# Row maxima of a two-layer cross attention: one turning product for both query halves, at another place in each slot

## Chip, cores and metric

The kernel runs on one core of one Trainium2 chip. The metric is the device time of one execution in microseconds (us). The kernel before took 1475.73 us in the median of three runs (1470.49 to 1479.28).

## What is computed

Two cross-attention layers follow each other over 16 sequences of 256 queries with 320 channels (20 heads of 16). Keys and values come from a context of 256 tokens with 512 channels, of which some are text tokens and some image tokens: 77 and 179 in layer 1, 252 and 4 in layer 2. Text and image have softmaxes of their own, so each query has a row maximum for each part and head.

```python
def layer1(x, ctx, mask):                          # text = ctx[:, :77], ip = ctx[:, 77:]
    q = x @ Wq                                     # [16, 256, 320], 20 heads of 16
    probs  = softmax(q_h @ k_text_h.T * scale)     # over the 77 text tokens, each head
    sem    = softmax(q @ k_text.T * scale) @ text @ ip.T * scale    # all heads together
    ip_p   = softmax(q_h @ k_ip_h.T * scale + 0.5 * sem) * mask     # over the 179 image tokens
    return (probs @ v_text_h + ip_p @ v_ip_h) @ Wout + bout + x

def layer2(x, ctx, mask):                          # text = ctx[:, :-4], ip = ctx[:, -4:]
    probs  = softmax(q_h @ k_text_h.T * scale)     # over the 252 text tokens
    qsem   = l2norm(probs @ text)                  # for each head
    ip_p   = softmax(q_h @ k_ip_h.T * scale + 0.5 * qsem @ l2norm(ip).T) * mask
    return (probs @ v_text_h + ip_p @ v_ip_h) @ Wout + bout + x

out = layer2(layer1(x, ctx, mask), ctx, mask)
```

## The kernel before

Four heads of one sequence are a group; there are 5 groups a sequence, so 80 groups in layer 1 (k from 0 to 79) and 80 in layer 2 (k from 80 to 159; NS is 80). The main loop runs over slots, one a group; a slot works on several groups at once, at different stages. Between its fixed steps a slot calls `fill`, which takes steps from other tasks (projections, keys, values, output) by a table of due times; these are the rows of the lines L260, L632, L690 and L1108.

A layer 1 slot k does, in this order on TensorE (PE):

- `maxima0(k + 1)`: the row maxima of the next group are turned so that they lie along a row. Each of the two halves of 128 queries has its own product with an identity matrix (L780), 8 rows by 128 columns. ScalarE (ACT) copies both halves into the tile `mt` (L782, 8 x 256), and a DMA on ACT's queue writes them into two rows of the group's stacked queries `Q` (L783).
- `score0(k + 2, 0)`: the scores of the first half (L772), and their row maxima on VectorE (DVE), one reduction for text and one for image (L773 and L774). They go to the tile `mn`. The scores' PSUM tile S exists once.
- `turned0(k, 0)`: the scores once more, keys on the rows, for half the keys (L795). The rows of `Q` with the maxima take part in this product, so that the maximum is subtracted in it. ACT takes the exponential (L798) and GpSimd (POOL) multiplies by the semantic factor (L801).
- a `fill`, then `attend0(k - 1)`: 24 products with the values of the group before (L833), each on a quarter of the array's columns.
- `score0(k + 2, 1)` and `turned0(k, 1)` for the second halves, then two more `fill`s. `stacks(k + 4, "KQ")` behind them has the SP queue load keys and queries of a later group (L83).

Layer 2 is alike. In slot k `both1(k, t)` does the probabilities of group k (L917, with the row of maxima in it) and the scores of group k + 2 (L922, maxima L923), for t = 0 and t = 1, with `attend1(k - 2)` (L988 and L990) between the two. Behind them come four blocks `norm1` (L975), `rounded1` (L965, L966) and the fills, and at the slot's end `maxima1(k + 2)`: two products (L955), a copy (L957) and a DMA (L959).

PE's order is the order in which the program is written. In layer 1 a scheduler sets the order on ACT, DVE, POOL and the SP queue, within the few fixed orders that `queued` and `anchor` add; `turned0` has the second half's exponentials queued behind the DMA of the next group's maxima, and `stacks(..., "M")` has a copy queued behind the latest copy of maxima. In layer 2 ACT, DVE and POOL follow the program too. `bank()` gives one of three PSUM banks (X) in turn.

Of the kernel before, what the change touches and what calls it, by code (L numbers as in the profile page):

```python
# [9 lines left out]
FR = mybir.dt.float32r  # L10
AF = mybir.ActivationFunctionType
ALU = mybir.AluOpType
AX = mybir.AxisListType
# [4 lines left out]
S = 256  # L18
# [6 lines left out]
T0 = 77  # L25
NIP = 4
BI = B * NIP
T1 = S - NIP
# [21 lines left out]
def xattn2(  # L50
# [39 lines left out]
    def bank(tag="X"):  # L90
        return ps.tile([128, 512], F32, tag=tag, name=tag, bufs=BANKS[tag])
# [83 lines left out]
    def anchor(inst):  # L175
        anchors[inst.ins.engine] = inst
        return inst
# [587 lines left out]
    def score0(k, t):  # L765
        Q, K = QK[k]
        if t == 0:
            maxes[k] = buf("mn", [128, 2, 2, 4], FR, bufs=2)
        mn = maxes[k]
        sp = scores()  # L770
        for h in range(4):
            mm(sp[:, h], Q[: XROW + T0, h, t * 128 : (t + 1) * 128], K[: XROW + T0, h], start=True, stop=True)  # L772
        nc.vector.tensor_reduce(mn[:, t, 0], sp[:, :, :T0], axis=AX.X, op=ALU.max)  # L773
        anchor(nc.vector.tensor_reduce(mn[:, t, 1], sp[:, :, T0:], axis=AX.X, op=ALU.max))  # L774

    def maxima0(k, queue=nc.scalar):
        Q, mn = QK[k][0], maxes[k]
        mp = bank()
        for t in range(2):
            mm(mp[:8, t * 128 : (t + 1) * 128], mn[:, t].rearrange("p a h -> p (a h)"), ident_r, start=True, stop=True)  # L780
        mt = buf("mt", [8, S], FR)
        casts.append(nc.scalar.copy(mt, mp[:8, :S]))  # L782
        issues[k] = queue.dma_start(f(Q[KS0 - 2 : KS0]), f(mt))  # L783

    def turned0(k, t):
# [17 lines left out]
    def attend0(k):  # L803
        b, g = divmod(k, NG)
        v, pv = get("v0", b), bank("P")
        for vt in range(3):
            values0(k, pv, v, vt)
        settle0(b, g, pv)

    def slot0(k):  # L810
        if k > 0:
            yield lambda: maxima(k + 1)
            yield lambda: stacks(k + LEAD - 1, "M")
        yield lambda: ahead(k + 2, 0)
        yield lambda: turned0(k, 0)
        yield 0.2
        if k == 2:
            yield lambda: stacks(k + LEAD - 1, "KQ")
        if k > 0:
            yield lambda: attend0(k - 1)  # L820
            yield lambda: stacks(k + LEAD - 1, "T")
        yield lambda: ahead(k + 2, 1)
        yield lambda: turned0(k, 1)
        if k != 1:
            yield lambda: stacks(k + LEAD, "KQ")
        yield 0.6
        yield 1.0
# [75 lines left out]
    def both1(k, t):  # L903

        a = k + 2 < 2 * NS and QK[k + 2] 
        c = NS <= k < 2 * NS and QK[k]
        if a:
            if t == 0:
                maxes[k + 2] = buf("mn", [128, 4, 4], FR, bufs=2)[:, :2]
            sp = scores()  # L910
        if c:
            st = [bank("T").rearrange("p (h t) -> p h t", h=2) for u in range(2)]
            lo = (0, DUP)[t]
            for j in range(2):
                for u in range(2):
                    rows = slice(64 * u, 64 * u + KS1)
                    mm(st[u][:, j], c[1][rows, j, lo : lo + 128], c[0][rows, j], start=True, stop=True)  # L917
        if a:
            for j in range(2):
                for u in range(2):  # L920
                    rows = slice(64 * u, 64 * u + XROW)
                    mm(sp[:, 2 * u + j], a[0][rows, j, t * 128 : (t + 1) * 128], a[1][rows, j], start=True, stop=True)  # L922
            anchor(nc.vector.tensor_reduce(maxes[k + 2][:, t], sp[:, :, :T1], axis=AX.X, op=ALU.max))  # L923
            image_scores(k + 2 - NS, t, sp)
        if c:
            for u in range(2):
                if t == 0:
                    P[k, u] = buf("P", [128, 2, 2, S], bufs=SIZES["NP"]) if (k - NS) % 3 else last_stack([128, 2, 2, S], F32, u)
                anchor(nc.scalar.activation(P[k, u][:, t], st[u], AF.Exp, scale=SCALE))  # L929
# [20 lines left out]

    def maxima1(k):
        mn = maxes[k]
        mp = bank()
        for t in range(2):
            mm(mp[:4, t * 128 : (t + 1) * 128], mn[:, t], ident_r, start=True, stop=True)  # L955
        mt = buf("mt", [8, S], FR)[:4]
        nc.scalar.copy(mt, mp[:4, :S])  # L957
        row = QK[k][0].rearrange("(u p) j t -> u p j t", u=2)[:, XROW]
        late(lambda: nc.scalar.dma_start(f(row), f(mt)))  # L959

# [32 lines left out]
    def slot1(k):  # L993
        last = k - 1 if NS < k <= 2 * NS else None
        mine = k < 2 * NS
        if k == NS:
            yield lambda: maxima(k + 1)
        yield lambda: both1(k, 0)
        if k == NS:
            yield lambda: attend0(k - 1)  # L1000
# [2 lines left out]
            yield lambda: summed.append(attend1(k - 2))  # L1003
        yield release
        yield lambda: both1(k, 1)
        if last:
            yield lambda: norm1(last, 0, 0)
        yield 0.2
# [14 lines left out]
        if mine:  # L1023
            yield lambda: rounded1(k, 1)
        yield 0.8
        yield lambda: maxima(k + 2)
        yield lambda: stacks(k + LEAD)
        yield 1.0

# [248 lines left out]
    def maxima(k):  # L1278
        if k < 2 * NS:
            (maxima0 if k < NS else maxima1)(k)  # L1280
# [189 lines left out]
```

## Time and profile before

| | |
|---|---|
| time before | 1475.73 us median of 3 runs (1470.49 to 1479.28) |
| the profiled execution | 1475.7 us, its span 1475.7 us |
| PE busy | 1433.6 us (97%), 12438 matmuls |
| DVE, POOL, ACT busy | 1166.0 us (79%), 1151.8 us (78%), 956.5 us (65%) |
| TensorE clock | granted in full in all 40 slices |
| DMA engines | busy 50.3% of the span for the SP queue's transfers, 0.2% for ACT's |

In the profile PE's rows are matmuls and PEld's their weight loads; a row gives the start, the length from the start of the first to the end of the last of the merged instructions, and how many these were. Matmuls are pipelined: the ends are modelled, and what one costs is read from the start of one to the start of the next. `[0.41 <-issue]` at a row's end is idle time of that engine ahead of it, and what ended it. ACTq and SPq rows are DMAs that these engines issue; q10 is ACT's DMA queue.

### The profile page before, as it was taken

Reading aid. Unit: us, or ns where it says so; the run is one execution under the profiler, and the core shown is the slowest. Engines: PE = TensorE matmul, PEld = TensorE weight load, DVE = VectorE, ACT = ScalarE, POOL = GpSimd, SP = SyncE. Lnnn points to the kernel's source line nnn. Section 1 sums busy time; section 2 is a strip of 40 time slices with the busy share of each in tenths; the row PEclk is TensorE's granted clock in tenths of the full one; section 3 lists DMA queues with packets and bytes.
Section 4 is the critical chain, followed back from the end, with each engine's and each line's share of the span. In section 5 each row is a group of like instructions: output and inputs, shape, how many; then the busy total and the mean of one; then the engine's idle time right before and its main releaser. Section 6 shows DMA issues by size and latency. Waiting matters only on the chain.

```text
span 1475.7 us, 35302 instructions
## 1 busy us (share of the span) xinstructions
PE 1433.6 (97%) x12438; PEld 1186.7 (80%) x12438; DVE 1166.0 (79%) x2569; ACT 956.5 (65%) x2074; POOL 1151.8 (78%) x1173
## 2 busy tenths in 40 slices
PE   6899999999999999799999999999999999999998
PEld 6788888888888878687778887888888888888865
DVE  5487676777677787967888888888888888888897
ACT  5577676767676776756666566656665666566553
POOL 4179797979797877987788877787778877887785
PEclk9999999999999999999999999999999999999999
DMA  6756565656656577565434433543354345433511
GB/s 196 194 160 184 134 184 141 184 143 165 162 154 164 144 195 205 140 184 158 138 102 140 146 119 101 161 146 102 118 161 146 89 131 161 135 101 116 150 32 50
DMA packets 230667, 211.78 MB, mean 144 GB/s; under 512 B 56314, under 2 KB 217116, under 8 KB 230492
## 3 DMA queue, kind: packets, MB, share of 16 engines
q1 hardware_dynamic: 229222, 208.56, 50.3%
q8 instruction: 99, 1.62, 0.5%
q10 hardware_dynamic: 1270, 0.98, 0.2%
q14 instruction: 76, 0.62, 0.1%
HBM read 122.07 MB, written 86.44 MB: 141 GB/s over the span
## 4 chain that ended last, share of the span: by engine, by line
PE 86%; DMA 4%; DVE 3%; POOL 3%; ACT 2%; issue 1%; SPq 0%; ACTq 0%; DVEq 0%; POOLq 0%
PE X L260 22%; PE X L975 18%; PE X L632 11%; PE P L833 7%; PE S L772 5%; PE P L988 5%; PE T L917 5%; PE T L795 4%; PE S L922 3%; PE P L990 2%; DMA kd<-kst 2%; PE X L1108 1%; POOL P L801 1%; PE X L690 1%; POOL wt L966 1%
## 5 line engine op out<-in xcount | busy, mean ns | idle before, releaser
L801 POOL TENSOR_TENSOR P<-P,rs 128x512 f32<-128x512 f32 x320 | 413.6, 1316 | 140.2 <-ACT P L798 140.2
L975 PE MATMUL X<-ctb,gm 128*128 128x512 f32 x1120 | 295.3, 407 | 0.0
L966 POOL TENSOR_TENSOR wt<-P,ctb 128x512 f32<-128x512 f32 x212 | 268.6, 1296 | 0.0
L923 DVE TENSOR_REDUCE mn<-S 128x4 fp32r<-128x1008 f32 x160 | 192.8, 1205 | 81.0 <-PE S L922 79.4
L975 PEld LDWEIGHTS X<-ctb,gm 128*128 128x128 f32 x1120 | 203.6, 190 | 49.4 <-issue 0.4
L798 ACT ACTIVATE P<-T 128x512 f32<-128x512 f32 x320 | 174.7, 593 | 100.5 <-PE T L795 81.0
L978 DVE TENSOR_TENSOR wt<-X,wt 128x512 f32<-128x512 f32 x240 | 159.3, 681 | 4.9 <-PE X L975 4.9
L929 ACT ACTIVATE P<-T 128x512 f32<-128x512 f32 x212 | 115.0, 597 | 54.5 <-PE T L917 41.6
L980 POOL TENSOR_TENSOR wt<-wt 128x512 f32<-128x512 f32 x80 | 103.6, 1295 | 58.3 <-DVE wt L978 58.3
L965 ACT ACTIVATE ctb<-P 128x512 fp32r<-128x512 f32 x212 | 122.5, 625 | 32.7 <-PE X L975 31.1
L774 DVE TENSOR_REDUCE mn<-S 128x4 fp32r<-128x716 f32 x160 | 142.4, 890 | 0.0
L833 PE MATMUL P<-P,vr 128*32 128x256 f32 x1920 | 123.8, 387 | 1.8 <-DVE tmp L850 0.8
L632 PE MATMUL X<-hq,wE 128*128 128x256 f32 x768 | 111.1, 289 | 4.4 <-ACT hq L615 3.9
L260 PE MATMUL X<-cta,wA 128*128 128x252 f32 (+3 forms) x726 | 104.2, 289 | 6.9 <-ACT wA L187 6.8
L632 PE MATMUL X<-ho,wF 128*128 128x256 f32 x768 | 106.6, 284 | 0.9 <-DVE ho L871 0.6
L632 PEld LDWEIGHTS X<-hq,wE 128*128 128x128 f32 x768 | 101.6, 195 | 7.2 <-ACT hq L615 4.4
L260 PEld LDWEIGHTS X<-cta,wA 128*128 128x128 f32 (+1 forms) x726 | 94.4, 191 | 10.7 <-ACT wA L187 7.0
L632 PEld LDWEIGHTS X<-ho,wF 128*128 128x128 f32 x768 | 98.7, 189 | 3.9 <-DVE ho L871 1.0
L844 DVE STREAM_TRANSPOSE nt<-P 128x512 f32<-128x512 f32 x80 | 57.0, 713 | 44.2 <-PE P L833 43.9
L773 DVE TENSOR_REDUCE mn<-S 128x4 fp32r<-128x308 f32 x160 | 74.5, 466 | 21.5 <-PE S L772 21.1
L833 PEld LDWEIGHTS P<-P,vr 128*32 128x32 f32 x1920 | 55.7, 110 | 42.7 <-issue 6.0
L772 PE MATMUL S<-ks,qs 125*128 125x256 f32 x480 | 87.0, 304 | 0.9 <-DVE mn L774 0.8
(223 smaller groups left out, 3279.7 us busy)
## 6 DMA issues: line engine op xcount, KB each, us to landing
qd<-q SPq DMA_DIRECT2D x48, 384.0 KB
kd<-kst SPq DMA_DIRECT2D x66, 256.0 KB
rawc<-in_cT_dram SPq DMA_DIRECT2D x60, 256.0 KB
qs<-qd SPq DMA_DIRECT2D x160, 96.0 KB
ks<-kd SPq DMA_DIRECT2D x160, 96.0 KB
qs<-qd SPq DMA_DIRECT2D x60, 192.0 KB
ks<-kd SPq DMA_DIRECT2D x60, 192.0 KB
qd<-q SPq DMA_DIRECT2D x32, 256.0 KB
```

The source lines that it names most:

```text
L260: last = mm(out, lhs(a, k), rhs(b, k), start=i == 0, stop=i == len(terms) - 1)
L632: mm(pp, w(s, k, slice(m * 128, (m + 1) * 128)), a[:, t], start=i == 0, stop=i == len(terms) - 1)
L772: mm(sp[:, h], Q[: XROW + T0, h, t * 128 : (t + 1) * 128], K[: XROW + T0, h], start=True, stop=True)
L774: anchor(nc.vector.tensor_reduce(mn[:, t, 1], sp[:, :, T0:], axis=AX.X, op=ALU.max))
L798: exp = anchor(nc.scalar.activation(pt, st[p], AF.Exp, scale=SCALE))
L801: anchor(nc.gpsimd.tensor_mul(pt, pt, rs[:, t : t + 1].to_broadcast([128, 2, S])))
L833: mm(pv[32 * s : 32 * s + 32, o : o + S], v[:, vt, h : h + 32], P[k, s // 2][:, t, s % 2], start=vt < 2, stop=vt != 1,)
L923: anchor(nc.vector.tensor_reduce(maxes[k + 2][:, t], sp[:, :, :T1], axis=AX.X, op=ALU.max))
L965: nc.scalar.activation(R[k, u][:, t], P[k, u][:, t], AF.Copy, scale=0.5)
L966: anchor(nc.gpsimd.tensor_sub(W[k, u][:, t], P[k, u][:, t], f(R[k, u][:, t])))
L975: mm(yp, gm[:, gb], R[k, u][:, kt], start=i == 0, stop=i == len(blocks[n]) - 1)
L978: nc.vector.tensor_mul(product, yp, w[:, n])
```

## The change

The maxima tile gets the half of the queries as its last index, so that both halves' maxima lie next to each other. One product turns both: 16 rows by 128 columns in layer 1, 8 by 128 in layer 2, in place of two products of 8 and of 4 rows. The copy has 128 columns instead of 256 on twice the rows, and the DMA twice as many rows of half the length (16 of 512 bytes in layer 1). In layer 1 `maxima(k + 1)` moves from the head of slot k to the place directly behind `attend0(k - 1)`, past the first scores, the first probabilities and a fill. In layer 2 the maxima of group k + 1 are turned in slot k directly behind `both1(k, 1)`; before, they were turned at the end of slot k - 1.

```diff
     def score0(k, t):
...
-            maxes[k] = buf("mn", [128, 2, 2, 4], FR, bufs=2)
+            maxes[k] = buf("mn", [128, 2, 4, 2], FR, bufs=2)
...
-        nc.vector.tensor_reduce(mn[:, t, 0], sp[:, :, :T0], axis=AX.X, op=ALU.max)
-        anchor(nc.vector.tensor_reduce(mn[:, t, 1], sp[:, :, T0:], axis=AX.X, op=ALU.max))
+        nc.vector.tensor_reduce(mn[:, 0, :, t], sp[:, :, :T0], axis=AX.X, op=ALU.max)
+        anchor(nc.vector.tensor_reduce(mn[:, 1, :, t], sp[:, :, T0:], axis=AX.X, op=ALU.max))
 
     def maxima0(k, queue=nc.scalar):
         Q, mn = QK[k][0], maxes[k]
-        mp = bank()
-        for t in range(2):
-            mm(mp[:8, t * 128 : (t + 1) * 128], mn[:, t].rearrange("p a h -> p (a h)"), ident_r, start=True, stop=True)
-        mt = buf("mt", [8, S], FR)
-        casts.append(nc.scalar.copy(mt, mp[:8, :S]))
+        mp = bank()[:16, :128]
+        mm(mp, mn.rearrange("p a h t -> p (a h t)"), ident_r, start=True, stop=True)
+        mt = buf("mt", [16, 128], FR)
+        casts.append(nc.scalar.copy(mt, mp))
         issues[k] = queue.dma_start(f(Q[KS0 - 2 : KS0]), f(mt))
 
     def slot0(k):
         if k > 0:
-            yield lambda: maxima(k + 1)
             yield lambda: stacks(k + LEAD - 1, "M")
...
             yield lambda: attend0(k - 1)
+            yield lambda: maxima(k + 1)
             yield lambda: stacks(k + LEAD - 1, "T")
...
     def maxima1(k):
         mn = maxes[k]
-        mp = bank()
-        for t in range(2):
-            mm(mp[:4, t * 128 : (t + 1) * 128], mn[:, t], ident_r, start=True, stop=True)
-        mt = buf("mt", [8, S], FR)[:4]
-        nc.scalar.copy(mt, mp[:4, :S])
+        mp = bank()[:8, :128]
+        mm(mp, mn.rearrange("p c t -> p (c t)"), ident_r, start=True, stop=True)
+        mt = buf("mt", [8, 128], FR)
+        nc.scalar.copy(mt, mp)
...
     def slot1(k):
...
-        if k == NS:
-            yield lambda: maxima(k + 1)
         yield lambda: both1(k, 0)
...
         yield lambda: both1(k, 1)
+        yield lambda: maxima(k + 1)
...
         yield 0.8
-        yield lambda: maxima(k + 2)
         yield lambda: stacks(k + LEAD)
```

Behind the change the line numbers are one to four lower (L779 for L780, L794 for L795, L832 for L833; L916, L921, L953 and L973 for L917, L922, L955 and L975). PE's order in one layer 1 slot, before: from the last values of group k - 1 (L833, `v` on `P`) to the next slot's probabilities (L795, on the queries `qs_188`). L772 are scores into S, L690 is a fill's step, L780 turns the maxima.

```order
L833 MATMUL P<-P_93,vr 32x256 x2
L833 MATMUL P<-P_94,vr 32x256 x2
L772 MATMUL S<-ksl,qsl 128x256 x4
L795 MATMUL T<-qs_187,ks_191 128x256 x4
L690 MATMUL X<-kb_238,q_297 128x192 x12
L780 MATMUL X<-ident_r,mn_556 8x128 x2
L772 MATMUL S<-ks_190,qs_186 128x256 x4
L795 MATMUL T<-qs_188,ks_192 128x256 x4
```

The same place on PE after the change:

```order
L832 MATMUL P<-P_93,vr 32x256 x2
L832 MATMUL P<-P_94,vr 32x256 x2
L779 MATMUL X<-ident_r,mn_555 16x128
L772 MATMUL S<-ksl,qsl 128x256 x4
L794 MATMUL T<-qs_187,ks_191 128x256 x4
L690 MATMUL X<-kb_238,q_297 128x192 x12
L772 MATMUL S<-ks_190,qs_186 128x256 x4
L794 MATMUL T<-qs_188,ks_192 128x256 x4
```

The product that fills the maxima row of `qs_188` stood a slot's length ahead of the probabilities that read it; it now stands behind the values, with the second half's scores and probabilities, the fill and one more block of scores between.

ACT's order in the same slot, before: P are exponentials, `qs_186<-tph` and `ks_191<-M` copies for later groups, `mt` the turned maxima.

```order
L782 CAST mt_196<-X 8x256
L744 CAST ks_190<-M_333 77x4x179
L798 ACTIVATE P_95<-T 128x512
L783 DMA qs_188<-mt_196 2x4x256
L798 ACTIVATE P_96<-T 128x512
L741 CAST qs_186<-tph_449 77x1024
L798 ACTIVATE P_95<-T 128x512
L798 ACTIVATE P_96<-T 128x512
```

After, the same rows on ACT:

```order
L744 CAST ks_190<-M_333 77x4x179
L445 ACTIVATE M_332<-X 77x179
L429 ACTIVATE vr<-X,tmask 128x20x16
L797 ACTIVATE P_95<-T 128x512
L797 ACTIVATE P_96<-T 128x512
L741 CAST qs_186<-tph_449 77x1024
L781 CAST mt_196<-X 16x128
L782 DMA qs_188<-mt_196 2x8x128
L797 ACTIVATE P_95<-T 128x512
L797 ACTIVATE P_96<-T 128x512
```

The copy of the maxima and its DMA have gone from ahead of the first half's exponentials to between the first half's and the second half's, behind the copy of `tph`.

PE in a layer 2 slot, before, from the second scores (L922) to the next slot's probabilities (L917); L975 are the blocks of `norm1`:

```order
L922 MATMUL S<-ks_190,qs_186 128x256 x4
L975 MATMUL X<-ctb_82,gm 128x512 x4
L632 MATMUL X<-hq_293,wE_85 128x256 x8
L975 MATMUL X<-ctb_82,gm 128x512 x3
L975 MATMUL X<-ctb_83,gm 128x512 x7
L955 MATMUL X<-ident_r,mn_555 4x128 x2
L260 MATMUL X<-cta_80,wA_84 128x252 x6
```

And after:

```order
L921 MATMUL S<-ks_190,qs_186 128x256 x4
L953 MATMUL X<-ident_r,mn_556 8x128
L973 MATMUL X<-ctb_82,gm 128x512 x4
L632 MATMUL X<-hq_293,wE_85 128x256 x8
L973 MATMUL X<-ctb_82,gm 128x512 x3
L973 MATMUL X<-ctb_83,gm 128x512 x7
L260 MATMUL X<-cta_80,wA_84 128x252 x6
```

The pair has left the stream of full-array products at the slot's end, and the one product that is left stands where the array changes from the 48-row products L921 to full ones.

More of the change, by code (lines that the diff above doesn't have):

```diff
@@ L908, in both1 @@
             if t == 0:
-                maxes[k + 2] = buf("mn", [128, 4, 4], FR, bufs=2)[:, :2]
+                maxes[k + 2] = buf("mn", [128, 4, 2], FR, bufs=2)
             sp = scores()
@@ L922, in both1 @@
                     mm(sp[:, 2 * u + j], a[0][rows, j, t * 128 : (t + 1) * 128], a[1][rows, j], start=True, stop=True)
-            anchor(nc.vector.tensor_reduce(maxes[k + 2][:, t], sp[:, :, :T1], axis=AX.X, op=ALU.max))
+            anchor(nc.vector.tensor_reduce(maxes[k + 2][:, :, t], sp[:, :, :T1], axis=AX.X, op=ALU.max))
             image_scores(k + 2 - NS, t, sp)
```

## Prediction

> **What bounds the kernel now.** I read the page first, then the groups by line and shape, the waits, and the timeline of a slot in each layer. On the page, the span and the chain of work that ended last:
>
> ```profile
> span 1475.7 us, 35302 instructions
> ...
> PE 86%; DMA 4%; DVE 3%; POOL 3%; ACT 2%; issue 1%; SPq 0%; ACTq 0%; DVEq 0%; POOLq 0%
> ```
>
> 86% of the chain is PE: what is taken out of PE's stream comes off the time, unless a wait takes its place. The groups of the turning products, by line and shape:
>
> ```profile
> L780 PE MATMUL X<-ident_r,mn 128*8 128x128 f32 x160 | 24.8, 225 | 5.1 <-DVE mn L774 3.7 <-DMA kd<-kst 0.3 <-DVE ho L871 0.3
> ...
> L955 PE MATMUL X<-ident_r,mn 128*4 128x128 f32 x160 | 22.9, 223 | 0.6 <-DVE kst L564 0.6
> ```
>
> There are 160 of each, 80 pairs a layer. Their means of 0.22 us are modelled ends; what a pair costs is in the starts. PE's timeline at the end of a layer 2 slot and in the next:
>
> ```profile
> 1004.15 0.28 PE L955 MATMUL X<-ident_r,mn 128*4 128x128 f32 x2
> 1004.27 2.12 PE L632 MATMUL X<-ho,wF 128*128 128x256 f32 x16
> 1006.23 1.12 PE L632 MATMUL X<-hq,wE 128*128 128x256 f32 x8
> ...
> 1011.08 1.11 PE L632 MATMUL X<-hq,wE 128*128 128x256 f32 x8
> 1012.03 2.49 PE L975 MATMUL X<-ctb,gm 128*128 128x512 f32 x10
> ```
>
> In a stream, eight L632 take 1012.03 - 1011.08 = 0.95, so 0.119 us each. The pair takes 1004.27 - 1004.15 = 0.12, and the sixteen L632 behind it 1006.23 - 1004.27 = 1.96 where 16 x 0.119 = 1.90: their first weights wait behind the small ones. A pair thus costs 0.12 + 0.06 = 0.18 us.
>
> **The change part by part.** *One product for two, and its new place.* The slot of layer 1 that the order shows, in the timeline:
>
> ```profile
> 316.94 1.50 PE L833 MATMUL P<-P,vr 128*32 128x256 f32 x24
> ...
> 317.30 1.03 ACT L741 CAST qs<-tph 77x1024 fp32r<-77x1024 f32 x1
> 318.37 0.54 PEld L772 LDWEIGHTS S<-ksl,qsl 125*128 125x128 f32 x4 [0.41 <-issue]
> 318.37 0.74 PE L772 MATMUL S<-ksl,qsl 125*128 125x256 f32 x4
> ...
> 318.95 0.64 PE L795 MATMUL T<-qs,ks 127*128 127x256 f32 x4
> ...
> 319.45 1.09 ACT L798 ACTIVATE P<-T 128x512 f32<-128x512 f32 x2 [1.12 <-PE T L795]
> ...
> 319.62 0.30 SPq L83 DMA_DIRECT2D ks<-kd  x1
> ...
> 320.13 2.54 POOL L801 TENSOR_TENSOR P<-P,rs 128x512 f32<-128x512 f32 x2 [0.59 <-ACT P L798]
> ...
> 320.75 0.28 PE L780 MATMUL X<-ident_r,mn 128*8 128x128 f32 x2
> ...
> 321.07 0.36 ACT L782 CAST mt<-X 8x256 fp32r<-8x256 f32 x1
> ...
> 321.39 0.64 PE L795 MATMUL T<-qs,ks 127*128 127x256 f32 x4
> ...
> 321.46 0.62 ACTq L783 DMA_DIRECT2D qsl<-mt  x1
> ...
> 322.91 0.85 PE L833 MATMUL P<-P,vr 128*32 128x256 f32 x12
> ```
>
> Behind the values the weight path stands still for 0.41 us while the array changes over, and the scores then start with an exposed load. The product now stands in that gap. No row has it there. The nearest is a pair whose second half waited for DVE, so that its load started on a weight path that stood idle:
>
> ```profile
> 307.25 0.09 PEld L780 LDWEIGHTS X<-ident_r,mn 128*8 128x8 f32 x1 [0.34 <-DVE mn L774]
> 307.32 0.53 PEld L772 LDWEIGHTS S<-ks,qs 125*128 125x128 f32 x4
> ```
>
> The scores' load follows 0.07 us after the small one; alone it would have started at 307.25. I take 0.07 for the product there. The bounds are 0 (it fits into the 0.41) and half a pair in the stream and all of the load's delay, 0.06 + 0.06 = 0.12. In layer 2 the place is of the same kind, since there too a full load follows products that use part of the array, and I take 0.07 again. A slot saves 0.18 - 0.07 = 0.11 us, at the bounds 0.06 and 0.18.
>
> *Where the saving doesn't count.* Rows of the waits, then of what the probabilities of layer 2 wait for:
>
> ```profile
> PEld S L772 <- issue: 30.5, 73, 0.8
> ...
> PEld X L780 <- DVE mn L774: 7.4, 11, 1.7
> ...
> PE T L795 <- DMA qs<-mt: 4.6, 1, 4.6
> ...
> PE X L780 <- DVE mn L774: 3.7, 4, 1.4
> ```
>
> ```profile
>   ACT P L929: 6.2, 15
>   DVE sr L939: 5.3, 13
> ```
>
> The first row says that the gap behind the values is there in 73 slots. In 11 + 4 = 15 slots the pair waited for the reduction L774. The scores behind it write the PSUM tile S, which exists once and which that reduction reads, so the wait stays and changes its name to the scores': nothing is saved there. In layer 2, 15 + 13 = 28 slots start with a wait for ACT or DVE, and I count them as nothing too. Layer 1: 65 x 0.11 = 7.2 us. Layer 2: 52 x 0.11 = 5.7 us. Together 12.9 us, at the bounds 117 x 0.06 = 7 and 117 x 0.18 = 21.
>
> The Trainium skill ("TensorE: Matmul & The Clock Gate", section "LDWEIGHTS (loading the stationary operand)") has a load take its number of columns divided by 1.2 GHz, 0.013 us for 16 columns; by that the product would cost some 0.02 us in the gap and the sum would come to an estimated 117 x 0.16 = 19 us. The trace doesn't bear it out for small loads: 8 columns show 0.09 us, and the next load 0.07 later.
>
> *The later transfer in layer 1.* This is what speaks against the change. The maxima of the next group were on their way a whole slot ahead; now the chain product, copy, issue, landing has to fit between the values and the next slot's probabilities. In the slot above the product starts at 318.37. ACT's copy of `tph`, which the order puts ahead, ends at 317.30 + 1.03 = 318.33 and is out of the way. Copy: 0.32 after the first product as at 321.07, so 318.69, and 0.36 long at most (half the columns). Issue: 0.39 after the copy's start as at 321.46, so 319.08. The landing is seen in ACT's queue q10. All ten of its packets of the issue at 321.46 lie in the window from 321.46 to 322.95:
>
> ```profile
> q10 hardware_dynamic: 10, 0.01, 1.6%
> ```
>
> That is 1.49 us at most, so the row is there at 320.57; twice the rows of half the length I put at 0 to 0.2 more. It is read by L795, which would start at 321.39 - 0.18 + 0.07 = 321.28. So 0.5 to 0.7 us are left. Of the 77 slots that I followed from the values to the next slot's probabilities, 18 are about as tight (2.9 to 3.0 us from scores to probabilities), the first and the last of them with these probabilities:
>
> ```profile
> 157.13 0.64 PE L795 MATMUL T<-qs,ks 127*128 127x256 f32 x4
> ```
>
> ```profile
> 628.26 0.64 PE L795 MATMUL T<-qs,ks 127*128 127x256 f32 x4
> ```
>
> The others have 3.1 us or more, most of them over 4. But a landing takes longer when the DMA engines are full. For this issue the ten packets lie in the window from 362.40 to 363.30, 3.0 to 3.9 us after it:
>
> ```profile
> 359.41 0.62 ACTq L783 DMA_DIRECT2D qs<-mt  x1
> ```
>
> ```profile
> q10 hardware_dynamic: 10, 0.01, 3.1%
> ```
>
> The engines' load where the new transfer would run, in the slot above and in the tight slot half a period later (the column before the last is the DMA share):
>
> ```profile
> 318.90:320.90 2.00, 2.00 (x21) 2.00 (x20) 1.92 (x6) 1.20 (x3) 1.41 (x2) 1.00 0.11 29
> ...
> 356.40:358.40 2.00, 2.00 (x21) 2.00 (x20) 1.88 (x5) 1.45 (x3) 2.00 (x3) 1.00 0.93 293
> ```
>
> The first kind is idle, the second full. Of the 18 tight slots about six are like the second. A landing between the two rows, 2.9 us, comes 319.08 + 2.9 - 321.28 = 0.7 us late: 6 x 0.7 = 4.2 us lost. At the bounds 0, and with 3.9 us 6 x 1.7 = 10.
>
> The Trainium skill ("DMA: Bandwidth & Descriptors", section "Queues, rings and completion order") has each DMA engine take its queues in turn, a packet of each; by that a small transfer would hardly wait for the SP queue's backlog and these 4.2 us would be none. The row of 3.0 us and more speaks against it, and I keep 4.2.
>
> *ACT and those behind it.* Between the halves ACT now has the copy and the issue, behind which the second half's exponentials are queued. The issue ends at 319.08 + 0.62 = 319.70, or 319.9 if more rows take longer; the exponentials start then and not at 319.45. POOL's products follow 0.25 to 0.45 later and end at 320.13 + 2.54 + 0.45 = 323.1 at the latest. They are read by the last third of the next values, which start at 322.91 and take 1.50, so at 323.9: 0.8 us are left, and this costs nothing. The first half's exponentials no longer have the copy and the issue ahead of them.
>
> *Layer 2's transfer.* The second scores, the exponentials of that half, and the next slot's probabilities:
>
> ```profile
> 1009.72 0.40 PE L922 MATMUL S<-ks,qs 48*128 48x256 f32 x4
> ...
> 1009.92 1.09 ACT L929 ACTIVATE P<-T 128x512 f32<-128x512 f32 x2 [1.02 <-PE T L917]
> ...
> 1016.01 0.51 PE L917 MATMUL T<-qs,ks 49*128 49x256 f32 x4
> ```
>
> ACT copies behind the exponentials, at 1011.0, issues at 1011.4, and even 3.9 us land at 1015.3, ahead of 1016.0. It costs nothing. The bank that the product takes comes free with the copy at 1011.4, before the third product behind it wants it.
>
> **The sum.** 1475.7 - 12.9 + 4.2 = 1467.0 us; the span and the execution's own time are the same 1475.7, which is also the median of the runs, so nothing is added.
>
> **The rivals.**
> *The landing takes it all back.* If all 18 tight slots wait 0.7 us, because twice the rows need longer or the copy on ACT starts late, the loss is 12.6 us and the time 1475 (1471 to 1479). For it: the one wait of 4.6 us for such a transfer that is there already, and a slack of 0.5. Against: the idle engines in the first kind of slot.
> *Slower: the transfer collides with the next loads.* SP issues the keys of a later group at 319.62, 0.5 us behind the moved issue, and the queries behind them. If the moved issue slips behind them by 0.55 us, its packets stand in the load of these two in every tight slot, a landing of up to 3.9 comes 1.4 us late on the mean, and 18 x 1.4 = 25 us are lost: 1475.7 - 12.9 + 25 = 1488. It decides at an issue later than 319.62 in this slot. Against: the copy of `tph` ends before the product is there.
> *More saved.* If the small product fits into the gap altogether, 21 us come off and with the landings 1459.
> That the change doesn't do what it says would be a PE stream that keeps its length because DVE's reductions are next everywhere. The 15 + 28 slots with such waits are taken out of the sum already; it lies within the first rival.
>
> **How the numbers follow.** A measurement of this kernel can tell about 0.5% (7.4 us) from no change. Chances: the forecast 0.46 (1461 to 1472), more saved 0.12, taken back 0.24, slower 0.18. Under 1468.3 lie three quarters of the forecast, 0.35, and the second, 0.12: faster 0.47. Same: 0.11 of the forecast and 0.22 of the third: 0.33. Slower: the last and 0.02: 0.20. The cases of both signs make the range 1457 to 1483, the forecast's own is 1461 to 1472.
>
> **What would show it.** In the profile after: 80 products L779 and 80 L953 in place of 320; the weight path's wait ahead of the scores moved to the small load; scores that wait for L774 in about 15 slots; waits of L794 for the DMA `qs<-mt` of 4 us in sum, in some six slots. It is wrong if these waits come to over 10 us, if the values wait for POOL, or if small loads behind the values cost more than 0.12 us.

## The result: slower, and the profile after

The changed kernel takes 1521.32 us in the median of 4 runs (1512.44 to 1532.9), the kernel before 1476.59 beside it. The ratio is 1.0308 with a 95% interval from 1.0277 to 1.034: slower by 3%, where 1467.0 was forecast and 1483 was the upper end. The profiled execution took 1517.65 us, its span 1515.8.

The page of the changed kernel, span and chain of work that ended last, and the groups of the products:

```profile
span 1515.8 us, 34953 instructions
...
PE 79%; DVE 7%; DMA 7%; issue 3%; ACT 2%; POOL 1%; SPq 0%; ACTq 0%; DVEq 0%; POOLq 0%
```

```profile
L779 PE MATMUL X<-ident_r,mn 128*16 128x128 f32 x80 | 18.8, 235 | 0.0
...
L953 PE MATMUL X<-ident_r,mn 128*8 128x128 f32 x80 | 18.2, 228 | 0.0
```

The 320 products have become 160, and PE is not idle ahead of any of them. But PE's share of the chain fell from 86% to 79%, while DVE's and the DMAs' grew: waits have come into PE's stream. Where they are is seen first from the times of the copies of `mt`, one a slot (the view of this tile gives for each line the copies' shortest, median and longest time in ns and the start of the first and the last), before and after:

```profile
L782 ACT CAST mt<-X x80: 342/358/365, 49.2 to 659.7; 8x256 fp32r<-8x256 f32 x80
L957 ACT CAST mt<-X x80: 339/357/367, 667.5 to 1438.2; 4x256 fp32r<-4x256 f32 x80
```

```profile
L781 ACT CAST mt<-X x80: 238/254/257, 49.5 to 671.0; 16x128 fp32r<-16x128 f32 x80
L955 ACT CAST mt<-X x80: 235/238/255, 678.1 to 1481.7; 8x128 fp32r<-8x128 f32 x80
```

Layer 1 ends 671.0 - 659.7 = 11 us later. Layer 2 takes 1481.7 - 678.1 = 803.6 us from first copy to last and took 770.7: 33 us more. The waits of PE and of its weight path (PEld) that are new or have grown, us in total, times, longest:

```profile
PEld X L260 <- DVE wt L978: 24.3, 13, 1.9
...
PE X L260 <- DVE wt L978: 19.0, 13, 1.5
...
PEld X L779 <- issue: 14.8, 35, 0.8
...
PE T L794 <- DMA qs<-mt: 11.5, 11, 3.3
...
PEld T L794 <- ACT sp L692: 9.0, 5, 2.8
PEld X L1104 <- DVE wt L976: 8.2, 13, 0.7
...
PEld X L632 <- DVE wt L976: 6.1, 12, 0.5
...
PE T L794 <- DMA qsl<-mt: 1.5, 2, 1.3
```

The third row is the gap behind the values, which now stands ahead of the small load as forecast. The two rows of PE on L794 are layer 1's probabilities waiting for the rows of maxima, 11.5 + 1.5 = 13.0 us. The row of PEld on L794 names ACT, but it is the same standstill, seen on the weight path: in these five slots the transfer is the last to come, as is shown below. The three on L260, L1104 and L632 come 12 or 13 times, about once a sequence, all in layer 2: 24.3 + 8.2 + 6.1 = 38.6 us of weight path. One such place in layer 2, changed kernel:

```profile
1008.52 0.23 PE L953 MATMUL X<-ident_r,mn 128*8 128x128 f32 x1
...
1008.58 3.44 PE L973 MATMUL X<-ctb,gm 128*128 128x512 f32 x14
...
1011.86 0.59 PE L1104 MATMUL X<-rs,rs 128*128 128x256 f32 x2
...
1012.71 0.70 PE L1104 MATMUL X<-rs,rs 128*128 128x256 f32 x2 [0.26 <-DVE wt L976]
...
1013.41 0.69 DVE L976 TENSOR_TENSOR X<-X,wt 128x512 f32<-128x512 f32 x1
...
1014.14 0.69 DVE L978 TENSOR_TENSOR wt<-wt,X 128x512 f32<-128x512 f32 x1
...
1014.88 2.03 PE L260 MATMUL X<-wC,cta 128*128 128x320 f32 x12 [1.47 <-DVE wt L978]
```

And the same place before:

```profile
988.27 3.48 PE L975 MATMUL X<-ctb,gm 128*128 128x512 f32 x14
...
991.60 1.02 PE L1108 MATMUL X<-rs,rs 128*128 128x256 f32 x4
...
992.27 2.09 PE L260 MATMUL X<-wC,cta 128*128 128x320 f32 x12
...
993.90 0.69 DVE L980 TENSOR_TENSOR wt<-wt,X 128x512 f32<-128x512 f32 x1
```

The values of a later group (L260 with `wC`) read nothing that DVE's add writes. Before, they start 4.00 us after the first `norm1` block, and the add starts 1.63 us after them. In the changed kernel they start 0.05 us after the add ends (1014.14 + 0.69 = 1014.83), 6.30 us after the first block. What ties them to the add is the PSUM bank. Here the text on record was wrong: `bank()` does not give three banks in turn. When the kernel is built, every PSUM tile, whatever its tag, gets one of all eight banks. The built programs list them; for the two L1104 tiles and the value tile at this place, the same in all 13 sequences:

```
              first L1104            second L1104               L260, wC
before        bank 1, after scores   bank 2, after L917's T     bank 3, after L917's T (freed by ACT L929)
changed       bank 4, after maxima   bank 2, after third norm1  bank 3, after fourth norm1 (freed by DVE L978)
```

In layer 2 as a whole 104 tiles of the changed kernel take a bank of the third PSUM tile before them in PE's order; in the kernel before 1 does. (The texts on record below count 91 in the changed kernel, 53 in `l2_pbank` and 1 in `one_old`; counted tile by tile in the built programs it is 104, 60 and 6.)

Layer 1, one of 16 slots in which the probabilities stand still ahead of L794 (changed kernel):

```profile
201.68 0.09 PEld L779 LDWEIGHTS X<-ident_r,mn 128*16 128x16 f32 x1 [0.41 <-issue]
201.69 0.23 PE L779 MATMUL X<-ident_r,mn 128*16 128x128 f32 x1
201.70 0.53 PEld L772 LDWEIGHTS S<-ks,qs 125*128 125x128 f32 x4
201.75 0.69 PE L772 MATMUL S<-ks,qs 125*128 125x256 f32 x4
...
201.96 0.25 ACT L781 CAST mt<-X 16x128 fp32r<-16x128 f32 x1 [0.73 <-PE X L779]
...
202.24 0.62 ACTq L782 DMA_DIRECT2D qsl<-mt  x1
...
202.95 0.31 SPq L83 DMA_DIRECT2D ks<-kd  x1
...
203.31 0.43 SPq L83 DMA_DIRECT2D qs<-qd  x1
...
206.01 0.71 PE L794 MATMUL T<-qsl,ksl 127*128 127x256 f32 x4 [1.28 <-DMA qsl<-mt]
```

In the window from 202.24 to 204.89 ACT's queue q10 has all 18 packets of this transfer, beside SP's q1:

```profile
q1 hardware_dynamic: 533, 0.65, 86.4%
q10 hardware_dynamic: 18, 0.01, 1.1%
```

The issue comes 0.55 us after the product, quicker than the 0.71 of the forecast. The last packet is through 2.65 us later, and PE starts only 1.12 us after that. Over the 16 slots PE starts 0.45 to 1.47 us after the last packet, and the standstills (what is over 0.25 us from the start before to L794's) add up to 14.6 us. The trace also keeps the updates of the semaphore, the counter by which a reader learns that a transfer is there; no view of the profile prints them. In all 16 slots this transfer's last update comes 0.41 to 1.34 us behind its last packet. In 15 of them PE starts 0.04 to 0.14 us behind that update, also where the view names ACT; in the other one (at 566.49) the reduction L774, which frees the bank, ends 0.2 us behind it.

### The profile page after: what moved, and what is told of

It reads as the page before. It is cut to its first block, busy times and chain, and to the rows that moved or that the text cites. A ratio compares the mean times of both kernels' runs of the same rounds, so it can differ in the third digit from the quotient of the medians.

```text
span 1515.8 us, 34953 instructions
## 1 busy us (share of the span) xinstructions
PE 1431.4 (94%) x12278; PEld 1173.0 (77%) x12278; DVE 1186.2 (78%) x2569; ACT 944.3 (62%) x2074; POOL 1151.1 (76%) x1173
## 4 chain that ended last, share of the span: by engine, by line
PE 79%; DVE 7%; DMA 7%; issue 3%; ACT 2%; POOL 1%; SPq 0%; ACTq 0%; DVEq 0%; POOLq 0%
PE X L260 21%; PE X L973 15%; PE X L632 10%; PE P L832 7%; PE P L986 5%; PE T L794 4%; PE T L916 4%; PE S L772 4%; DMA qs<-mt 3%; PE S L921 3%; PE P L988 2%; DVE wt L976 1%; DMA rawc<-in_cT_dram 1%; PE X L690 1%; DVE u L1056 1%
## 5 line engine op out<-in xcount | busy, mean ns | idle before, releaser
L973 PE MATMUL X<-ctb,gm 128*128 128x512 f32 x1120 | 289.4, 401 | 0.6 <-DVE wt L976 0.3
L922 DVE TENSOR_REDUCE mn<-S 128x4 fp32r<-128x1008 f32 x160 | 192.7, 1204 | 71.4 <-PE S L921 71.4
L973 PEld LDWEIGHTS X<-ctb,gm 128*128 128x128 f32 x1120 | 201.7, 189 | 39.6 <-ACT qsl L928 0.7
L774 DVE TENSOR_REDUCE mn<-S 128x4 fp32r<-128x716 f32 x160 | 142.6, 891 | 0.0
L832 PE MATMUL P<-P,vr 128*32 128x256 f32 x1920 | 123.7, 390 | 1.8 <-DVE tmp L849 1.1
L632 PE MATMUL X<-hq,wE 128*128 128x256 f32 x768 | 109.8, 288 | 6.4 <-ACT hq L615 3.5
L632 PE MATMUL X<-ho,wF 128*128 128x256 f32 x768 | 112.0, 290 | 3.4 <-DVE ho L872 1.2
L632 PEld LDWEIGHTS X<-ho,wF 128*128 128x128 f32 x768 | 101.0, 193 | 14.5 <-DVE wt L976 6.1
L260 PE MATMUL X<-cta,wA 128*128 128x252 f32 (+3 forms) x726 | 104.4, 290 | 8.2 <-ACT wA L187 6.3
L632 PEld LDWEIGHTS X<-hq,wE 128*128 128x128 f32 x768 | 101.6, 194 | 9.4 <-ACT hq L615 4.1
L260 PEld LDWEIGHTS X<-cta,wA 128*128 128x128 f32 (+1 forms) x726 | 96.1, 192 | 14.4 <-ACT wA L187 6.5
L260 PE MATMUL X<-wC,cta 128*128 128x320 f32 x480 | 82.5, 319 | 19.0 <-DVE wt L978 19.0
L794 PE MATMUL T<-qs,ks 127*128 127x256 f32 x480 | 80.1, 290 | 15.9 <-DMA qs<-mt 11.5
L616 POOL TENSOR_TENSOR hq<-xq,hq 128x512 fp32r<-128x512 f32 x29 | 38.8, 1339 | 72.8 <-ACT hq L615 72.8
```

Of the source, the lines that this page charges most:

```text
L260: last = mm(out, lhs(a, k), rhs(b, k), start=i == 0, stop=i == len(terms) - 1)
L632: mm(pp, w(s, k, slice(m * 128, (m + 1) * 128)), a[:, t], start=i == 0, stop=i == len(terms) - 1)
L774: anchor(nc.vector.tensor_reduce(mn[:, 1, :, t], sp[:, :, T0:], axis=AX.X, op=ALU.max))
L794: mm(st[p][:, j], K[:KS0, 2 * p + j, t * 128 : (t + 1) * 128], Q[:KS0, 2 * p + j], start=True, stop=True)
L832: mm(pv[32 * s : 32 * s + 32, o : o + S], v[:, vt, h : h + 32], P[k, s // 2][:, t, s % 2], start=vt < 2, stop=vt != 1,)
L922: anchor(nc.vector.tensor_reduce(maxes[k + 2][:, :, t], sp[:, :, :T1], axis=AX.X, op=ALU.max))
```

## Experiments

Theory B: layer 2's loss is the bank that the moved product takes and the other choice of banks that comes with it. Theory L: layer 1's loss is the landing. Rivals: the merged product itself (M), its place behind products on part of the array (P), or the copy and issue in mid-slot (D). Each label's time stands against runs of the kernel before on the same chip, with the ratio's 95% interval.

**Parts alone.** `one_old`: the merged product at the old places. `one_l1new` and `one_l2new`: the new place in one layer alone. `two_new`: the old pair at the new places.

The edit of `one_old` against the changed kernel (`one_l1new` has its second half alone, `one_l2new` its first, `two_new` moves the pair the other way in the kernel before):

```diff
     def slot0(k):
         if k > 0:
+            yield lambda: maxima(k + 1)
...
             yield lambda: attend0(k - 1)
-            yield lambda: maxima(k + 1)
...
     def slot1(k):
+        if k == NS:
+            yield lambda: maxima(k + 1)
...
         yield lambda: both1(k, 1)
-        yield lambda: maxima(k + 1)
...
         yield 0.8
+        yield lambda: maxima(k + 2)
```

> One product for two, but at the old places in both layers. Theory B (banks): in the changed kernel layer 2's PE waits because PSUM banks come round sooner at the new place; at the old place the built program has 1 bank in layer 2 that is taken again as the third tile after it (the changed kernel 91, the kernel before 1), so no such wait, and one small product less in each of some 145 slots at 0.06 us: 1476.6 - 9 = 1468 (1463 to 1473). Theory P (the place: a small product behind products that use part of the array costs PE more than a pair in the stream): the old place is kept, the same 1468. Theory M (the merged product itself, its sixteen or eight columns, or the wider rows of its transfer, is what costs): slower than 1476.

> One product for two; the new place in layer 1 alone, the old one in layer 2. From the two traces layer 1 is 11 us longer in the changed kernel and layer 2 33 us. B and P alike: 1476.6 + 11 - 5 = 1483 (1478 to 1489), with the waits of the probabilities for the transfer near 11 us as in the changed kernel. If layer 1's loss was only a shift between the layers: 1470 or less.

> One product for two; the new place in layer 2 alone, the old one in layer 1. B: the built program has the same 91 banks taken again as the third tile as the changed kernel, so the same waits of L260, L1104 and L632 for DVE (24 + 8 + 6 us): 1476.6 + 33 - 5 = 1505 (1499 to 1511). P: the same, but without these waits, the time in the steps behind L953. Neither: 1468.

> The old pair of products at the new places in both layers: the move without the merge. B: the built program has the same 91 banks in layer 2 taken again as the third tile, so the loss is there without the merge, 1521 + 0.06 x 145 = 1530 less what stands inside the waits: 1521 to 1530. P: each small product behind tiled ones costs more than in the stream, so the pair about twice the loss: 1560. If the merge is the cause: near 1476.

| | time, us | ratio | layer 1's last copy | layer 2, first to last copy |
|---|---|---|---|---|
| before | 1476.26 | | 659.7 | 770.7 |
| one_old | 1477.11 | 1.0002 (0.999 to 1.0014) | 659.1 | 769.8 |
| one_l1new | 1495.58 | 1.0118 (1.0087 to 1.0148) | 674.0 | 771.9 |
| one_l2new | 1507.33 | 1.0195 (1.0175 to 1.0216) | 652.4 | 806.2 |
| two_new | 1528.95 | 1.0348 (1.0321 to 1.0374) | 673.3 | 810.5 |

M and the merge fall: the loss comes with the move, with one product or two, and each layer's place costs by itself. P as stated falls too: the pair at the new places costs 8 us more than the single product, not twice the loss. `one_old` missed its 1468: the merge alone brings nothing. `one_l1new` lost 12 us more than I had put down, and its waits show where: 16.4 + 2.9 = 19.3 us for the transfer, in 12 slots, against 3.1 in one slot of `one_old`. (That one slot is the layer's first, whose transfer goes over the SP queue in all these kernels; it waits 4.6 us in the kernel before and 3.6 in `one_l1new`.) In `one_l2new` the wait of the changed kernel comes back to the digit. The rows of the waits in these two:

```profile
PE T L794 <- DMA qs<-mt: 16.4, 10, 3.6
...
PE T L794 <- DMA qsl<-mt: 2.9, 2, 2.1
```

```profile
PE X L260 <- DVE wt L978: 19.0, 13, 1.5
```

**Layer 2: the same order, another bank.** `l2_pbank` is `one_l2new`, and `after_pbank` the changed kernel, with the product written into columns 384 to 511 of the values' PSUM tile, which is live at that place and doesn't use them (three slots at the layer's start have no such tile and keep `bank()`).

```diff
-    def maxima1(k):
+    def maxima1(k, *into):
         mn = maxes[k]
-        mp = bank()[:8, :128]
+        mp = into[0][:8, 384:512] if into else bank()[:8, :128]
...
-        yield lambda: maxima(k + 1)
+        yield lambda: maxima(k + 1, *[s[2] for s in summed])
```

> one_l2new (1507), but in layer 2 the product is written into unused columns of the values' PSUM tile, which is live there anyway, so that the product takes no bank of its own; no table, banks chosen when the program is built. Place, copy, transfer and order are one_l2new's. In the built program 53 banks of layer 2 are taken again as the third tile after it (one_l2new 91, the kernel before 1), and none of them by L260 behind DVE's add L978. B: L260's 24 us of wait and most of the rest go, 1507 - 30 = 1477 (1470 to 1485). P or D: 1505.

> The changed kernel with one thing changed: layer 2's product is written into unused columns of the values' PSUM tile, as in l2_pbank. Theory B (layer 2's loss is the bank that the product takes) and L (layer 1's is the landing) add up: l2_pbank 1472.8 plus one_l1new - one_old = 1495.6 - 1477.1 = 18.5, so 1491 (1485 to 1497), 30 us under the changed kernel, with layer 1 as long as there (some 671 us to the last copy of mt) and its waits for DMA qs<-mt. If the two places hurt each other: 1500 or more.

`l2_pbank` took 1472.77 us (10 runs), `after_pbank` 1486.71 (ratio to before 1.008, 1.0054 to 1.0107). All five engines of `l2_pbank` have their instructions in the order of `one_l2new`; place, copy, issue and transfer are the same. 1507.33 - 1472.77 = 34.6 us are gone, and 1521.32 - 1486.71 = 34.6 from the changed kernel. Layer 2 takes 771.5 us in both. The same place as above in `l2_pbank`:

```profile
987.40 3.44 PE L973 MATMUL X<-ctb,gm 128*128 128x512 f32 x14
...
990.68 1.02 PE L1104 MATMUL X<-rs,rs 128*128 128x256 f32 x4
...
991.36 2.10 PE L260 MATMUL X<-wC,cta 128*128 128x320 f32 x12
...
992.97 0.69 DVE L978 TENSOR_TENSOR wt<-wt,X 128x512 f32<-128x512 f32 x1
```

The values are again 3.96 us behind the first block and ahead of the add; the build has given them the bank of L916's T, as before. That is theory B, shown for the 33 us. What is left of such waits in `l2_pbank`:

```profile
PEld X L260 <- DVE wt L976: 8.6, 15, 0.6
```

`l2_pbank` is faster than both kernels: its ratio to before is 0.9976 (0.9962 to 0.9989), some 3.5 us. These don't lie in layer 2, which is 0.8 us longer than before; 1.5 us are gone at the end of layer 1 and 3.5 behind the last copy, so what brings them is open.

**Layer 1: the work without the wait.** `l1_again` is `one_old` with layer 1's product, a copy and a transfer done a second time at the new place, into a buffer that nobody reads (`again0`: the product, ACT's copy, a DMA on ACT's queue).

```diff
             yield lambda: attend0(k - 1)
+            yield lambda: again0(k + 1)
```

> one_old (1477) with layer 1's product done a second time at the new place, with a copy on ACT and a transfer like the real one that nobody reads; the real ones stay at the old place. Theory L (landing): what layer 1 loses at the new place (15 us between one_old and one_l1new) is the probabilities' wait for the transfer, 17.8 us in 13 slots; here nobody waits for the second one, so only the product's own 0.07 us in 77 slots is added: 1477 + 5 = 1482 (1477 to 1487). Theory D (the copy and the issue stand ahead of the second half's exponentials on ACT, and POOL and the values follow late): 1477 + 15 or more = 1492.

1481.07 us, ratio 1.0036 (1.002 to 1.0052), where the same work waited for costs 1495.58. The probabilities (here L803) wait as `one_old`'s do:

```profile
PE T L803 <- DMA qs<-mt: 3.3, 1, 3.3
```

The product with all that hangs on it, unread, costs 1481.07 - 1477.11 = 4 us (5 were expected). The other 1495.58 - 1481.07 = 14.5 us come when somebody waits for the transfer: it is the landing, as theory L says and as the semaphore updates above show. D is tested in part only. In 69 of 78 slots the second copy and issue do stand between the two halves' exponentials on ACT, but this issue keeps ACT for 0.31 us and the real one for 0.62. What D would cost shows where the values' weights wait for POOL: 4.8 us in `one_l1new`, 2.4 in `l1_again`, 1.6 in `one_old`. So some 2 of the 14.5 us could be D's.

**Banks written into the kernel.** To change banks and nothing else I also replaced the build's choice by a table, one digit for each of the 2176 PSUM tiles. It took three forms, and the first two had a fault.

```diff
-        return ps.tile([128, 512], F32, tag=tag, name=tag, bufs=BANKS[tag])
+        i = int(next(plan))
+        return pair[:, 512 * i : 512 * i + 512] if i < 2 else single[i - 2][:, :]
```

First form, the bank longest free in the program's order, in all of the kernel:

> The changed kernel, but every PSUM tile gets its bank from a table written into the kernel (the bank that has been free longest) in place of the choice made when the program is built. In layer 2 all engines but SP keep the order of the changed kernel; no bank is taken again before the fifth tile after it, except by the wide scores tile. Theory B (banks): the waits of L260, L1104 and L632 for DVE go (24 + 8 + 6 us), and in layer 1 those of the probabilities for ACT's L692 (9 us): 1521 - 38 - 9 = 1474 (1467 to 1482). Theory P or D (the place, or the later copy and transfer): the order is the same, so the time stays at 1521, at best 1512.

> The kernel before with such a table: what the table is worth by itself. B: before had hardly a short reuse in layer 2, so little: 1476 (1468 to 1479). If the table alone brings as much here as in the changed kernel (30 us or more), it isn't the banks of the moved product that cost.

> One product for two at the old places, with such a table. Its steps show the product 0.06 us shorter in 145 of 160 slots, but the time was the same as before's. B: the built choice of banks took it back (waits for the copy of mt and for ACT that before doesn't have), so with the table before_plan's time less 9 us, about 1466. If it is again no faster than before_plan, what the product saves in PE's stream isn't on the path.

> One product for two, the new place in layer 1 alone, with such a table. Against one_old_plan: 77 slots x 0.05 us less in the stream = -4, and the waits of the probabilities for the transfer: my forecast had 4 us, the changed kernel showed 13. If the landing is the whole of layer 1's loss: one_old_plan + 4 to + 10. If layer 1's loss was banks too: one_old_plan - 4 to 0.

They took 1566.25, 1537.79, 1524.56 and 1508.62 us: 33 to 90 us over before, with the table's own waits in place of the old ones (in `after_plan` 38 us of `norm1` for ACT's copy of `ho`). `one_l1new_plan` came 16 us under `one_old_plan`, where theory L alone had asked for 4 to 10 above it; no run here says why. Second form, `after_built` with the changed kernel's own banks, the others with the banks longest free by the times of the trace, in layer 2 alone:

> A control. The changed kernel with the table of banks, and in the table the very banks that were chosen when the changed kernel was built (all but 3 of 2176 tiles). If writing the table costs nothing by itself, the changed kernel's time, 1521 (1512 to 1530), with its waits of L260 (24), L1104 (8) and L632 (6 us) for DVE in layer 2. If the table itself costs: slower, as the last four tables were.

> The same table, but in layer 2 each tile gets the bank that was free first by the times in the trace of the changed kernel (not by the order in the program, which the last tables went by). By that trace 17 of layer 2's X tiles take a bank that came free less than 0.3 us ahead or not yet, with the built banks 63. The order of PE, ACT and POOL in layer 2 is the same, and so is DVE's. Theory B: the 38 us of waits go, all or most: 1521 - 33 = 1488 (1480 to 1498), L260's wait for DVE's add under 5 us. Theory P or D (place, or the later copy and transfer): 1521.

> One product for two at the old places, with the built banks in layer 1 and the banks that were free first by its trace in layer 2. By the trace 9 tiles of layer 2 have less than 0.3 us, of which 2 are X, with the built banks 43. B: the built choice hid the 0.06 us a slot in layer 2, so 1477 - 5 = 1472 (1467 to 1476). If the saving in PE's stream isn't on the path: 1477.

> The kernel before with its built banks in layer 1 and in layer 2 those that were free first by its trace (11 tiles with less than 0.3 us, built 32). B: a little faster than before, 1472 (1467 to 1477). If it is slower by 10 us or more, such a table is no fair comparison for the others.

1538.09, 1553.23, 1516.1 and 1524.65 us. The control shows that the table itself costs 17 us. Line numbers are 28 higher in these kernels (L288 is L260), and tiles are called `one` and `pair`; the values' wait in `after_built` and in `after_t2`:

```profile
PE one L288 <- DVE wt L1006: 19.1, 13, 1.5
```

```profile
PE pair L288 <- ACT ho L907: 39.5, 13, 3.1
```

With the same banks the same wait is there. In `after_t2` the table had put the values into one bank of the scores' double tile and an L1104 tile into the other, and the build made the one wait for readers of the other. Third form, never two live tiles in that pair:

> The control with the changed kernel's own banks cost 17 us, and its trace shows what the tables had in common: the two banks of the scores' tile are one tile there, so a product in one half waits for readers of the other half (after_t2's 39.5 us of L260 waiting for ACT's copy of ho are of this kind). Here the table never has two live tiles in these two banks; layer 1 keeps the built banks, layer 2 takes those with the most time to spare by the trace of the changed kernel; the order of the engines in layer 2 is the changed kernel's. Theory B (banks): L260's wait for DVE's add (24 us) and those of L1104 and L632 (8 + 6) go, and the span from the first copy of mt in layer 2 to the last, 803.6 us in the changed kernel and 770.7 before, comes to 766 to 775. Theory P or D (the place, or the copy and the transfer): 800 or more.

> One product for two at the old places, with a table over both layers made as in after_t4 from its own trace. If the banks chosen when it was built took back the 0.06 us a slot that the single product saves: 1477 - 9 = 1468 (1462 to 1474), faster than before and after. If the saving isn't on the path: 1477. If the scores' two banks in one tile cost as in the earlier tables: 1485 or more.

`after_t4` took 1515.74 us, ratio 1.0261 (1.0212 to 1.0309). Its layer 2 has 787.4 us, half of the way: the wait for the add is gone, and another for a bank has come.

```profile
PE one L288 <- DVE ho L898: 17.8, 13, 1.4
```

`one_old_t4` took 1480.45, ratio 1.0015 (0.9994 to 1.0036); its layer 2 is the shortest of all, 762.7 us, its layer 1 10 us longer. As a proof of theory B the tables failed, and by the text of `before_t2`, which came out 49 us slower than before, the first two forms are no fair comparison at all. With PE's order the same, layer 2 takes 787 us in `after_t4` and 808 in `after_built`; the 822 of `after_t2` contain the waits that the double tile adds.

## Why the prediction was wrong, step by step

**The price of the product: put too high.** Behind the values the product starts after 0.309 us, as the scores did before, and the scores 0.070 later; 0.07 was forecast. But the scores' first step is shorter for it, 0.172 us in place of 0.223. From the last values to the probabilities a slot takes 0.906 us and took 0.888 (medians of 77 slots), so 0.018 is the whole price. In layer 2 `norm1` starts 0.063 later, its first step is shorter too (0.287 for 0.339), and 0.011 is left. The second product of a pair is worth 0.064: at the old place the steps from the row ahead of the product to the probabilities take 0.703 us in `one_old` and 0.767 before. From layer 1's first copy of `mt` to its last, all steps into the products and the scores took 122.8 us before and take 113.0 now, 9.8 less; 7.2 was forecast.

**That it comes off the time: not seen.** `one_old` has this saving in part, 160 times 0.06 us, and no gain; `l2_pbank` has layer 2's, and layer 2 is no shorter. Against before, the 4.8 us between the two products of a pair go from `one_old`'s layer 2, and 3.9 come back in the steps from the product to L260, L632 and L1104. In `l2_pbank`'s layer 2 the steps into the products and `norm1` take 17.1 us less than before, and the steps into L260 and L632 take 12.9 more: ahead of these the weight path waits 10.9 us there and 0.4 before, 8.6 of it the bank wait shown above. So in layer 2 most of what was taken out of PE's stream comes back as waits, which the prediction's first sentence allowed and its sum did not count. Whether it would come off with other banks (`one_old_t4`'s layer 2 says so, its layer 1 hides it) stays open.

**The landing in layer 1: the mechanism right, the term mis-sized.** 4.2 us were forecast with bounds of 0 and 10; from the starts it is 14.6. (Of the 13.0 in the waits, 3.3 are the layer's first slot, which is not new, and four of the slots are under the names of ACT and DVE.) It was put at 6 slots and 0.7 us; it came in 16 slots, 0.9 us each. Of the 18 tight slots five stand still, 5.9 us in all, not far from the forecast. The other eleven have 3.4 to 5.2 us of room in the trace of before and were not counted; they lose 8.7 us. The step that failed took the row to be there with the last packet. PE starts 0.45 to 1.47 us behind it; with a start at the last packet the 16 slots would stand still for 3.3 us in all. No view of before showed this time, but its trace has it: for the issue at 321.46 the last update of the semaphore comes after 2.12 us, 0.67 behind the last packet. By that, 0.1 us was left where 0.5 to 0.7 was put down. The forecast's own test, over 10 us of these waits, says wrong. The slower rival named the place, the next loads of SP, but asked for a later issue; it needs none, since in the slot above the loads are issued 0.71 us behind it and it still takes 2.65 us.

**"It costs nothing" in layer 2: this step turned the sign.** It rested on the sentence that the bank comes free with the copy, "before the third product behind it wants it", on three X banks in turn. The product's own bank did come free in time: in layer 2 no product waits for the copy of `mt`. What cost 33 us is that the other tiles were dealt other banks, and no rival had that. It was in reach: the built program lists the banks, and the DVE add that frees the fourth block's bank was in the trace of before, 1.63 us behind the values' start.

**ACT, POOL, layer 2's transfer: nearly right.** Layer 2's probabilities wait 0.7 us once for the transfer. `l1_again` prices ACT's work, product and all, at 4 us, with an issue half as long. The values' weight path waits for POOL 4.9 us in 9 slots, before 1.6 in 3; no cost was forecast.

**The sum.** From 1475.7 to 1515.8 the span grew by 40 us: layer 1's end is 11 later, layer 2 is 33 longer, and what lies between and behind is 4 shorter. With the bank's 34.6 us taken away 1486.7 is left, 20 over the forecast: 10 are the landing's (14.6 for 4.2). The other 9 are not worked out term by term; the saving in layer 2 that comes back in other steps belongs to them.

By the Trainium skill ("TensorE: Matmul & The Clock Gate", section "LDWEIGHTS (loading the stationary operand)") a load of 16 columns is short, and at the new place the trace agrees: the scores' load starts 0.02 us behind it (201.68 and 201.70). The 0.02 us that the prediction worked out from it, for a saving of 19 us, are nearer to the measured 0.018 than the 0.07 that the sum took.

By the Trainium skill ("DMA: Bandwidth & Descriptors", section "Queues, rings and completion order") engines take their queues in turn; by that the small transfer would hardly wait. It does wait: its 18 packets took 2.65 us from the issue beside 533 of the other queue. But most of this lies ahead of the first packet, which comes 2.23 us after the issue in the median of the 16 slots and 1.27 in the other slots. From the first packet to the end of the last it is 0.42 us and 0.27. So the trace does not show that the turns are at fault.

## What to carry to other kernels

When a product is moved, list which tile each PSUM bank held before, at the new place and at its neighbours, from the built program of before and after; if the tile that frees a bank is read late by a slow engine, the next tenant waits for it, whoever it is. If the moved result fits into unused columns of a tile that is live there anyway, it takes no bank of its own; here that gave the values their old bank back, though not every tile. And a transfer that gets half a slot in place of a whole one needs its landing under load, in the slots with more room too, and the time from the last packet to the reader's start. The packets of its queue don't show that time; the trace's semaphore updates do, and so does the row of an engine that waited.

## What was not expected of the hardware

A PE that waits for a transfer starts 0.45 to 1.47 us after the transfer's last packet in the trace, 16 times out of 16, and in 15 of these 0.04 to 0.14 us after the last update of its semaphore. Twice the rows of half the length made 18 packets of 10 (16 rows and 2 of 4 bytes, for 8 and 2) and left ACT's issue as long as before (0.62 us in layer 1, 0.52 in layer 2). A small product behind tiled products costs PE 0.018 us in layer 1 and 0.011 in layer 2, where the second of a pair at the old place costs 0.064: the gap of 0.41 us behind the values stays, ahead of the small load, but the step behind the small product is shorter by most of what it takes.
